# Layer 1's turned parts prepared ahead of its loop, and layer 3's third products in groups of nine blocks

## The chip, the core and the metric

The kernel runs on one core of one Trainium2 chip. The metric is the device time of one execution in microseconds; lower is better. Five engines run their own instruction streams beside each other: PE (matrix multiplication), DVE (vector), ACT (scalar functions), POOL (GpSimd) and SP, which here only issues DMAs. They wait for one another through semaphores.

## What is computed

Four graph layers over 3327 nodes (padded to 3328 = 26 blocks of 128) with 64 features, and one adjacency matrix `adj`; after each, `x = layernorm(x + layer(x))`. The kernel gets `adj` transposed, so a block is 128 rows of it. The two layers that the change touches:

```python
# layer 1
x_tan = _logmap0(x, C)
adj_att = jax.nn.sigmoid(x_tan @ att_W[:D] + att_b + (x_tan @ att_W[D:]).T) * adj
x_local = _logmap(x[:, None, :], x[None, :, :], C)
support_t = jnp.einsum('ij,ijd->id', adj_att, x_local)
return _proj(_expmap(x, support_t, C), C)

# layer 3
support = input @ weight
mask = (adj != 0).astype(support.dtype)
rank = jnp.cumsum(mask, axis=1)
deg = rank[:, -1:]
k = jnp.minimum(deg, float(MAX_NEIGH))
pos = rank - (deg - k)
w = mask * jnp.where(pos > 0, DECAY ** (k - pos), 0.0)
return w @ support + bias
```

## The kernel before

**Layer 1** (`near_sphere`, the arm that runs for this input). The distance of every pair of nodes comes from a product of two turned matrices: `ljT` (64 features on the partitions, nodes along the row; two copies, `ljT[1]` with the two halves of the partitions exchanged) and `riT`. Both are made by PE transposes into PSUM and a copy from there; `right` turns blocks of `lj` for `ljT[0]`, `turn` turns blocks of `ri` for `riT`, and `change_over` copies finished blocks of `ljT[0]` into `ljT[1]` by two DMAs on SP. A call such as `right, 1, 4` does blocks 1 to 4.

The loop runs over 104 tiles: two passes `cp` over the columns, 26 blocks `jb` in the order of `order`, two chunks `ci` of 2 x 416 columns. For a tile t, `products(t)` (L1103) writes four matmuls to a PSUM buffer `pq`, of which there are three, each of two banks; `linear(t)` lets DVE make `a` (L1115) from it and the attention `sg`, and ACT square it in place (L1116); `gather(t)` lets DVE make `v` (L1124), frees `pq` with that, issues `products(t + 3)` and adds v's product to an accumulator (L1136). Every second tile, `attention` lets ACT make a pair's sigmoids (L1076) and POOL multiply them with the adjacency block (L1088); SP loads that block (L1058, four buffers). Pass 0 also makes one block's factors on ACT per pair (`rows_of_sums`, L1230). The order on PE, ACT, DVE and POOL is the order of the program text (`manual_schedule`).

[...] Ahead of the loop six belong to single-use tiles (`alone`), and afterwards to the three `pq` buffers; two are the accumulators' (`bank(0, ...)`, `bank(1, ...)`), which serve for preparation first. Four parts are not prepared ahead but in the loop, at tiles 13 and 25: `gather` calls `prepare`, which takes the next `pq` buffer of the ring, does the transposes, and leaves the two copies to ACT one tile later.

**Layer 3** (in `layers`). Each step q is a block of one half h of the columns (52 steps, from the last block to the first). `masks` makes 0/1 masks on DVE three steps ahead (L341) from half a block each, loaded by SP into four buffers `ah` (L339). `advance` lets PE count neighbours along the blocks by four matmuls per c (L526); `read` turns the counts into weights `w`, for c = 0 on ACT (L541) and for c = 1 on DVE (L539). `products` multiplies w with the node features, which are split into three bf16 parts: the first two stand side by side in `s12` and take full-width matmuls (L722); the third, `s3`, is 64 columns wide, and its matmuls (L737) run in pairs, one for each half of the array's columns. The third products are not issued with each block: `later` collects blocks and issues them for `GROUP` = 3 blocks together, in the lines

```python
if last or c and len(later) == 2 * GROUP:
    for ql, cl in later:
```

At a half's last block, what is left is issued first for c = 0, then for c = 1. Until its third product is done, a block's w must stay; each c has `LEAD + GROUP + 2` buffers for it. `LEAD` = 3 is how many steps `products` stays behind `read`. The half's end (`sums_out`, `half_out`) normalises the first half's result on DVE and ACT, one part per step, beside the first steps of the second half.

Of the kernel before, what the change touches and what calls it, by code (L numbers as in the profile page):

```python
# [10 lines left out]
F32 = mybir.dt.float32  # L11
# [8 lines left out]
P = 128  # L20
N = 3327
NB = 26
# [41 lines left out]
CUBIC_PLUS = 2 * CUBIC_ROOT - 1  # L64
CUBIC_REST = 1.75705840270866
NEIGH = 100
GROUP = 3
LEAD = 3
AHEAD = 3
STEP = float(2**7)  # L70
# [6 lines left out]
def kernel(  # L77
# [819 lines left out]
    with tc.tile_pool(name="l1", bufs=1) as l1:  # L897
# [20 lines left out]
        with tc.tile_pool(name="l1a", bufs=1) as l1a, tc.tile_pool(  # L918
            name="l1ap", bufs=1, space=PSUM
        ) as l1ap:  # L920
            v = l1a.tile([P, NB], F32, name="v")
            sums = l1a.tile([P, NB], F32, name="sums")
# [26 lines left out]
            for i, g in enumerate(range(0, NBH, 4)):  # L949
                n = min(4, NBH - g)  # L950
# [60 lines left out]
        def near_sphere(mT, ljT_0, xm, sq_e, t_e, rows_63):  # L1011
# [3 lines left out]
            with tc.tile_pool(name="n1", bufs=1, reuse_waits="tile") as n1, tc.tile_pool(  # L1015
# [45 lines left out]

                orders = (order, sorted(order, key=lambda jb: jb in kept))
                tiles = [(cp, jb, ci) for cp in range(2) for jb in orders[cp] for ci in range(2)]
                us, pqs, a_s, accs, copies, sums = {}, {}, {}, {}, [], []

                def attention(pair):

# [26 lines left out]
                def products(t):  # L1094
                    if t >= len(tiles):
                        return
                    cp, jb, ci = tiles[t]
                    ch = 2 * cp + ci
                    of = slice(jb % NBH * P, (jb % NBH + 1) * P)
                    pq = n1q.tile([P, 2, 512], F32, tag="pq", name=f"pq_{t}")[:, :, :CW]  # L1100
                    for h in range(2):
                        rows = slice(h * D, (h + 1) * D)
                        nc.tensor.matmul(  # L1103
                            pq[:, h, :], ljT[h != jb // NBH][rows, of],
                            riT[rows, ch * CW : (ch + 1) * CW], start=True, stop=True,
                        )
                    pqs[t] = pq

                def linear(t):

                    if t >= len(tiles):
                        return
                    one = slice(slot(tiles[t][1]), slot(tiles[t][1]) + 1)
                    a_s[t] = n1w.tile(TW, F32, tag="a", bufs=3, name=f"a_{t}")
                    stt(a_s[t], pqs[t], CUBIC_PLUS, us.pop(t), op0=ALU.add, op1=ALU.mult)  # L1115
                    nc.scalar.activation(  # L1116
                        pqs[t], pqs[t], AF.Square, bias=al[:, one], scale=ga[:, one]
                    )

                def gather(t, extra=()):  # L1120

                    cp, jb, ci = tiles[t]
                    w = n1w.tile(TW, F32, tag="v", name=f"v_{t}")
                    stt(w, pqs.pop(t), CUBIC_REST, a_s.pop(t), op0=ALU.add, op1=ALU.mult)  # L1124
                    while sums:
                        sums.pop(0)()
                    if extra:
                        copies.extend(prepare(f"t{t}", extra))
                    if not extra:
                        products(t + 3)  # L1130
                    if jb == orders[cp][0]:
                        accs[cp, ci] = n1c.tile(
                            [P, CW], F32, tag=f"acc{ci}", name=f"acc1_{cp}_{ci}"
                        )
                    for h in range(2):
                        nc.tensor.matmul(  # L1136
                            accs[cp, ci][h * D : (h + 1) * D, :], xv[:, slot(jb), :], w[:, h, :],
                            start=(jb == orders[cp][0]), stop=(jb == orders[cp][-1]),
                        )
                    if extra:  # L1140
                        products(t + 3)
                    if jb == orders[cp][-1]:
                        of = slice((2 * cp + ci) * CW, (2 * cp + ci + 1) * CW)
                        sums.append(lambda: nc.scalar.copy(mT[:, of], accs[cp, ci]))
                        if t + 1 == len(tiles):
                            while sums:
                                sums.pop(0)()
# [43 lines left out]
                def change_over(b, n):  # L1191
                    of = slice(b * P, (b + n) * P)
                    nc.sync.dma_start(ljT[1][D:, of], ljT[0][:D, of])
                    nc.sync.dma_start(ljT[1][:D, of], ljT[0][D:, of])
# [7 lines left out]
                        )  # L1202
                    return riT[:, b * P : (b + n) * P], pt[:, : n * P]

                def prepare(name, parts):

                    pt = n1q.tile([P, 2, 512], F32, tag="pq", name=f"prep_{name}")
                    return [made(pt[:, k], *part) for k, part in enumerate(parts)]

                def made(pt, make, b, n):  # L1210
                    dst, src = make(pt, b, n)

                    def copy(to=nc.scalar.copy):
                        to(dst, src)
                        if make is right and b < 9:
                            change_over(b, n)

                    return copy

# [8 lines left out]
                def rows_of_sums(jb):  # L1228
                    sl = slot(jb)
                    nc.scalar.activation(  # L1230
                        xv[:, sl, : D - 1], xc[:, sl, : D - 1], AF.Copy, scale=gss[:, sl : sl + 1]
                    )

                def bank(which, make, b, n):

                    pt = n1c.tile([P, 4 * P], F32, tag=f"acc{which}", name=f"prep_{make.__name__}_{b}")
                    return made(pt, make, b, n)
# [3 lines left out]
                    pt = n1p.tile([P, 4 * P], F32, name=f"first_{make.__name__}_{b}")  # L1241
                    return made(pt, make, b, n)

                later = {13: ((right, 1, 4), (turn, 8, 4)), 25: ((right, 0, 1), (turn, 12, 1))}
                with tc.manual_schedule(
                    engines={
                        mybir.EngineType.PE, mybir.EngineType.Activation, mybir.EngineType.DVE,
# [49 lines left out]
                    n1q = pairs.enter_context(  # L1297
                        tc.tile_pool(name="n1q", bufs=3, space=PSUM, reuse_waits="tile")
                    )
                    by_rows = bank(1, left_rows, 0, NB)  # L1300
                    products(0)
                    products(1)
                    seventh = bank(0, right, 5, 4)
                    products(2)
                    list(attention(1))
                    rows_of_sums(order[0])
                    linear(0)
                    seventh()
                    list(attention(2))
                    for t in range(len(tiles)):  # L1310
                        linear(t + 1)
                        if t == 0:
                            by_rows()
                            rows_of_sums(order[1])
                        while copies:
                            copies.pop(0)()
                        gather(t, later.get(t, ()))
                        if t % 2 == 0:
                            list(attention(t // 2 + 3))
                            if t // 2 + 2 < NB:  # L1320
                                rows_of_sums(order[t // 2 + 2])
                        if t == 8:
                            spread_left(7)
                        if t == len(tiles) - 4:
                            of = slice(0, 2 * CW)
                            nc.gpsimd.tensor_tensor(xm[:, of], mT[:, of], ljT[0][:, of], ALU.mult)
                            gp = nc.gpsimd

                            gp.tensor_scalar(gs, g1, MIN_NORM, -256.0, ALU.max, ALU.mult)
                            gp.tensor_tensor(gk, gs, ga, ALU.mult)  # L1330
                            gp.tensor_scalar(gks, gk, -2.0, None, ALU.mult)
                            gp.tensor_tensor(gs2, gs, gs, ALU.mult)
                            gp.tensor_scalar(aav, aa, 1.0 / D, LN_EPS, ALU.mult, ALU.add)
                            gp.tensor_tensor(rows_63, but_last[:, :1], but_last[:, 1:], ALU.add)
                        if t == len(tiles) - 3:
                            pq = n1q.tile([P, 2, 512], F32, tag="pq", name="pq_early")
                            pm = pq[:, :, : 3 * (P + 2)].rearrange("p a (k w) -> p a k w", k=3)
                            for b in range(6):
                                nc.tensor.matmul(
                                    pm[:, b // 3, b % 3], mT[:, b * P : (b + 1) * P], all_m,  # L1340
                                    start=True, stop=True,
                                )
                        if t == len(tiles) - 2:
                            nc.scalar.activation(
                                sq_e.rearrange("p (a k h) d -> p a k (h d)", a=2, k=3),
                                pm[..., :P], AF.Square,
                            )
                            nc.scalar.copy(
                                t_e.rearrange("p (a k h) -> p a k h", a=2, k=3), pm[..., P:]
                            )  # L1350
# [521 lines left out]
```

## Time and profile before

| | us |
|---|---|
| median of 3 runs | 557.09 |
| lowest and highest | 556.18 and 557.86 |
| the profiled execution | 557.54 |
| its span in the profile | 555.7 |

| stage | us from the span's start |
|---|---|
| constants, layer 0 | 0 to 14 |
| layer 1: preparation | 14 to 22 |
| layer 1: loop of 104 tiles | 22 to 223 |
| layer 1: end | 223 to 241 |
| layer 2 | 241 to 394 |
| layer 3: node features, first steps | 394 to 409 |
| layer 3: steps, first half | 409 to 476 |
| layer 3: steps, second half | 476 to 541 |
| end | 541 to 556 |

Times in the profile are counted from the start of its span; 1.8 us of the execution lie outside it. A row of the time-ordered view has a start, a length, an engine, a line and what was written from what. PE's matmuls are pipelined, so the distance between two starts says what one costs, not its length. In brackets stands idle time of the engine before a row and what ended it.

### The profile page before, as it was taken

How to read it: one execution, taken by the hardware profiler on the slowest of the kernel's cores; microseconds unless marked ns; L12 is line 12 of the kernel's file. 1: busy time of each engine (PE TensorE's matmuls, PEld its weight loads, DVE VectorE, ACT ScalarE, POOL GpSimd, SP SyncE). 2: the span in 40 equal slices, each digit the busy share in tenths (PEclk: the TensorE clock that was granted, in tenths of full speed). 3: DMA queues.
4: the chain of work that ended last, by engine and by line, in shares of the span. 5: the costliest groups of instructions: out<-in, count | busy, mean ns of one | idle time of the engine just before them, and what ended most of it. 6: DMA issues, size and time to landing. Idle time of an engine off the chain costs nothing.

```text
span 555.7 us, 7392 instructions
## 1 busy us (share of the span) xinstructions
PE 527.5 (95%) x2841; PEld 226.9 (41%) x2841; DVE 372.2 (67%) x549; ACT 276.8 (50%) x325; POOL 207.4 (37%) x85
## 2 busy tenths in 40 slices
PE   8799989999999999999999999999999999999991
PEld 5422222222222222964444444434455555545541
DVE  6799999999999999798000011200678877887733
ACT  4899999999999997620000100000464333433321
POOL 3699999999999999000000000000001000000000
PEclk9889999999999999799999999999999999999996
DMA  8958866666667536799998049999029994799601
GB/s 282 365 205 288 257 209 225 210 223 220 225 232 243 187 123 247 277 416 425 423 427 367 1 163 424 426 426 399 6 66 344 329 326 167 246 296 349 247 1 38
DMA packets 33893, 143.57 MB, mean 258 GB/s; under 512 B 10269, under 2 KB 11959, under 8 KB 28855
## 3 DMA queue, kind: packets, MB, share of 16 engines
q1 hardware_dynamic: 31511, 142.40, 69.7%
q10 hardware_dynamic: 2336, 0.59, 0.5%
q8 instruction: 24, 0.39, 0.3%
q14 instruction: 22, 0.18, 0.1%
HBM read 141.53 MB, written 0.87 MB: 256 GB/s over the span
## 4 chain that ended last, share of the span: by engine, by line
PE 68%; DVE 17%; issue 7%; ACT 6%; POOL 1%; DVEq 0%; POOLq 0%; ACTq 0%
PE cnt L421 26%; PE cnt L526 11%; DVE v L1124 10%; PE pq L1103 9%; PE acc L722 6%; PE acc L1136 4%; PE acc L737 3%; ACT pq L1116 3%; ACT sg L1076 2%; DVE a L1115 2%; DVE w L539 1%; PE cnt L412 1%; DVE mask L341 1%; PE idle L928 1%; PE x_w L1455 1%
## 5 line engine op out<-in xcount | busy, mean ns | idle before, releaser
L1088 POOL TENSOR_TENSOR sg<-sg,at 128x1664 f32<-128x1664 f32 x44 | 163.7, 3738 | 3.7 <-ACT sg L1076 2.2
L1103 PE MATMUL pq<-riT,ljT 64*128 64x416 f32 x416 | 101.0, 564 | 11.6 <-DVE v L1124 7.9
L1116 ACT ACTIVATE pq<-pq,al,ga 128x832 f32<-128x832 f32 x104 | 104.6, 1012 | 12.1 <-DVE a L1115 12.0
L1115 DVE SCALAR_TENSOR_TENSOR a<-pq,sg 128x832 f32<-128x832 f32 x104 | 105.3, 1013 | 4.5 <-PE pq L1103 2.3
L1124 DVE SCALAR_TENSOR_TENSOR v<-pq,a 128x832 f32<-128x832 f32 x104 | 105.4, 1014 | 3.3 <-ACT pq L1116 2.2
L1136 PE MATMUL acc<-v,xv 128*64 128x416 f32 x416 | 96.0, 541 | 0.0
L1076 ACT ACTIVATE sg<-lb,rb 128x1664 f32<-128x1664 f32 (+1 forms) x53 | 87.3, 1649 | 0.0
L541 ACT ACTIVATE w<-cnt 128x832 int16<-128x832 f32 x55 | 47.3, 863 | 71.5 <-PE cnt L526 71.4
L421 PE MATMUL cnt<-at_l,lj 128*64 128x416 f32 x448 | 80.4, 513 | 0.0
L653 POOL TENSOR_TENSOR s<-sq,s 128x384 bf16<-128x384 f32 (+1 forms) x4 | 4.1, 1026 | 200.7 <-ACT s L652 200.7
L506 ACT ACTIVATE x<-cnt 128x416 f32<-128x416 f32 x8 | 4.1, 518 | 131.5 <-PE cnt L421 131.5
L539 DVE TENSOR_SCALAR w<-cnt 128x832 int16<-128x832 f32 x49 | 50.1, 1023 | 25.8 <-PE cnt L526 24.0
L1103 PEld LDWEIGHTS pq<-riT,ljT 64*128 64x128 f32 x416 | 31.7, 186 | 85.1 <-DVE v L1124 78.6
L526 PE MATMUL cnt<-mask,tri 128*128 128x416 bf16 x208 | 53.5, 339 | 0.1
L722 PE MATMUL acc<-w,s 128*128 128x416 bf16 x208 | 52.6, 339 | 0.5 <-DVE hid L794 0.5
L526 PE MATMUL cnt<-mask,rest 128*128 128x416 bf16 x200 | 51.6, 340 | 1.2 <-ACT w L541 0.6
L421 PEld LDWEIGHTS cnt<-at_l,lj 128*64 128x64 f32 x448 | 31.9, 137 | 46.2 <-issue 45.4
L1136 PEld LDWEIGHTS acc<-v,xv 128*64 128x64 f32 x416 | 20.7, 135 | 61.5 <-issue 57.8
L409 DVE COPY lj<-pn_l 128x512 f32<-128x512 f32 (+1 forms) x4 | 2.4, 592 | 61.6 <-PE pn_l L373 61.6
L341 DVE TENSOR_SCALAR mask<-ah 128x1664 bf16<-128x1664 f32 x42 | 43.4, 1034 | 0.0
L421 PE MATMUL cnt<-kept,lj 128*64 128x416 f32 x224 | 41.2, 513 | 0.0
L586 DVE TENSOR_TENSOR x<-x,xc 128x416 f32<-128x416 f32 x4 | 2.4, 588 | 41.5 <-ACT x L506 41.5
(285 smaller groups left out, 441.9 us busy)
## 6 DMA issues: line engine op xcount, KB each, us to landing
at_l<-in_adjT SPq DMA_DIRECT2D x24, 1664.0 KB, 12.8
at<-in_adjT SPq DMA_DIRECT2D x44, 832.0 KB, 4.9
ah<-in_adjT SPq DMA_DIRECT2D x42, 832.0 KB, 6.3
bt_l<-in_adjT SPq DMA_DIRECT2D x8, 1664.0 KB, 14.9
kept<-in_adjT SPq DMA_DIRECT2D x7, 1664.0 KB, 8.1
lb<-lf_rows SPq DMA_DIRECT2D x2, 384.0 KB, 6.1
ljT<-ljT SPq DMA_DIRECT2D x4, 128.0 KB, 5.5
x<-in_x ACTq DMA_DIRECT2D x1, 416.0 KB, 5.4
```

The source lines that it names most:

```text
L341: nc.vector.tensor_scalar(mask[q], at, 0.0, None, ALU.not_equal)
L421: nc.tensor.matmul(acc[c][h * D : (h + 1) * D, :], hw[:, slot(jb), :], blocks[jb][:, o : o + CW], start=c not in begun, stop=last, skip_gr ...
L526: nc.tensor.matmul(cnt[c][:, e, :], mat, mask[q][:, of], start=start, stop=(mat is tri), skip_group_check=True,)
L539: nc.vector.tensor_scalar(w.bitcast(I16), cnt[c], 0.0, None, ALU.max)
L722: nc.tensor.matmul(acc[h, c][:, e, :], s12[:, slot(jb)].rearrange("p t d -> p (t d)"), ws[q, c][:, e, :], start=first, stop=last,)
L1076: nc.scalar.activation(sg[:, :, of], lbs[:, :, of], AF.Sigmoid, bias=rb[:, sl : sl + 1])
L1088: nc.gpsimd.tensor_tensor(sg[:, :, of], sg[:, :, of], at[:, :, of], ALU.mult)
L1103: nc.tensor.matmul(pq[:, h, :], ljT[h != jb // NBH][rows, of], riT[rows, ch * CW : (ch + 1) * CW], start=True, stop=True,)
L1115: stt(a_s[t], pqs[t], CUBIC_PLUS, us.pop(t), op0=ALU.add, op1=ALU.mult)
L1116: nc.scalar.activation(pqs[t], pqs[t], AF.Square, bias=al[:, one], scale=ga[:, one])
L1124: stt(w, pqs.pop(t), CUBIC_REST, a_s.pop(t), op0=ALU.add, op1=ALU.mult)
L1136: nc.tensor.matmul(accs[cp, ci][h * D : (h + 1) * D, :], xv[:, slot(jb), :], w[:, h, :], start=(jb == orders[cp][0]), stop=(jb == orders[c ...
```

## The change

`GROUP` becomes 9, so that layer 3's third products are issued for nine blocks together, and each c has 14 buffers for w instead of 8.

In layer 1 the four parts that were prepared at tiles 13 and 25 are prepared ahead of the loop, and `prepare` and the `extra` path of `gather` go. `right, 0, 1` and `turn, 12, 1` share an accumulator's bank with the transposed row factors (`few`). `right, 1, 4` and `turn, 8, 4` take one `pq` buffer before the first product. All four are copied by DVE instead of ACT: `rows_1` and the two single blocks after `products(0)`, `rows_8` after `linear(0)`; `products(2)` moves behind it. Their `change_over` DMAs are issued at tiles 4 and 10.

```diff
-GROUP = 3
+GROUP = 9
...
-                def gather(t, extra=()):
+                def gather(t):
...
-                    if extra:
-                        copies.extend(prepare(f"t{t}", extra))
-                    if not extra:
-                        products(t + 3)
+                    products(t + 3)
...
-                    if extra:
-                        products(t + 3)
...
-                def prepare(name, parts):
-
-                    pt = n1q.tile([P, 2, 512], F32, tag="pq", name=f"prep_{name}")
-                    return [made(pt[:, k], *part) for k, part in enumerate(parts)]
-
-                def made(pt, make, b, n):
+                def made(pt, make, b, n, at_once=True):
                     dst, src = make(pt, b, n)
 
                     def copy(to=nc.scalar.copy):
                         to(dst, src)
                         if make is right and b < 9:
-                            change_over(b, n)
+                            if at_once:
+                                change_over(b, n)
+                            else:
+                                changes.append((b, n))
...
-                later = {13: ((right, 1, 4), (turn, 8, 4)), 25: ((right, 0, 1), (turn, 12, 1))}
...
-                    by_rows = bank(1, left_rows, 0, NB)
+                    few = n1c.tile([P, 4 * P], F32, tag="acc1", name="prep_few")
+                    by_rows = made(few[:, :P], left_rows, 0, NB)
+                    singles = [
+                        made(few[:, k * P : (k + 1) * P], make, b, 1, False)
+                        for k, make, b in ((1, right, 0), (2, turn, 12))
+                    ]
+
+                    fours_of = n1q.tile([P, 2, 512], F32, tag="pq", name="prep_fours")
+                    rows_1 = made(fours_of[:, 0], right, 1, 4, False)
                     products(0)
+                    rows_1(copy)
+                    for part in singles:
+                        part(copy)
+                    rows_8 = made(fours_of[:, 1], turn, 8, 4)
                     products(1)
                     seventh = bank(0, right, 5, 4)
-                    products(2)
                     list(attention(1))
                     rows_of_sums(order[0])
                     linear(0)
+                    rows_8(copy)
+                    products(2)
                     seventh()
                     list(attention(2))
                     for t in range(len(tiles)):
                         linear(t + 1)
                         if t == 0:
                             by_rows()
                             rows_of_sums(order[1])
-                        while copies:
-                            copies.pop(0)()
-                        gather(t, later.get(t, ()))
+                        gather(t)
...
+                        if t in (4, 10):
+                            change_over(*changes.pop(0))
```

## Prediction, before the run

> **What bounds the kernel now.** I read the page's slices first, then the time-ordered rows of each stage the change touches, then the waits there.
>
> ```profile
> PE   8799989999999999999999999999999999999991
> DVE  6799999999999999798000011200678877887733
> ACT  4899999999999997620000100000464333433321
> POOL 3699999999999999000000000000001000000000
> ```
>
> A slice is 13.9 us. Up to 222 us (layer 1) all four engines stand at nine tenths; afterwards only PE does. So layer 1 must be read by who waits for whom, and layer 3 (from 392 us) first as a sum of PE's slots.
>
> Layer 1, all engines around tile 13 (columns: start, us, engine, line, operation):
>
> ```profile
> 52.49 1.01 DVE L1115 SCALAR_TENSOR_TENSOR a<-pq,sg 128x832 f32<-128x832 f32 x1
> ...
> 52.63 0.65 PE L1175 MATMUL prep_t<-ident,lj 128*128 128x128 f32 x4
> ...
> 53.12 0.60 PE L1199 MATMUL prep_t<-ident,mT 128*128 128x128 f32 x4
> 53.61 1.02 DVE L1124 SCALAR_TENSOR_TENSOR v<-pq,a 128x832 f32<-128x832 f32 x1
> ...
> 54.48 0.59 ACT L1214 COPY ljT<-prep_t 128x512 f32<-128x512 f32 x1
> ...
> 54.69 1.89 PE L1103 MATMUL pq<-riT,ljT 64*128 64x416 f32 x8
> 54.96 0.59 ACT L1214 COPY riT<-prep_t 128x512 f32<-128x512 f32 x1
> ...
> 55.78 1.02 DVE L1115 SCALAR_TENSOR_TENSOR a<-pq,sg 128x832 f32<-128x832 f32 x1 [1.15 <-PE pq L1103]
> ```
>
> DVE runs a, v, a, v without a gap, 0.93 us apart, until `prep_t` takes the `pq` buffer that tile 16's products should have had. They go only at 54.69, after the next v has given up a buffer, and DVE stands 1.15 us. The same happens at 80.00 (1.13 us).
>
> Is something behind DVE that would keep it from going earlier? POOL:
>
> ```profile
> 131.88 70.75 POOL L1088 TENSOR_TENSOR sg<-sg,at 128x1664 f32<-128x1664 f32 x19 [0.52 <-ACT sg L1076]
> ```
>
> From 132 us on POOL multiplies without a gap, 3.72 us a pair, exactly DVE's pace (4 x 0.93).
>
> Layer 3, PE and then DVE:
>
> ```profile
> 430.86 0.52 PE L722 MATMUL acc<-w,s 128*128 128x416 bf16 x2
> 431.31 1.25 PE L737 MATMUL acc<-w,s 128*64 128x416 bf16 x12
> 432.49 0.52 PE L526 MATMUL cnt<-mask,rest 128*128 128x416 bf16 x2
> ```
>
> ```profile
> 485.20 1.07 DVE L798 TENSOR_REDUCE v_out<-sq 128x8 f32<-128x512 f32 x2
> 486.19 1.02 DVE L539 TENSOR_SCALAR w<-cnt 128x832 int16<-128x832 f32 x1
> ...
> 489.49 1.02 DVE L539 TENSOR_SCALAR w<-cnt 128x832 int16<-128x832 f32 x1
> ...
> 494.23 1.02 DVE L539 TENSOR_SCALAR w<-cnt 128x832 int16<-128x832 f32 x1
> 495.16 1.02 DVE L341 TENSOR_SCALAR mask<-ah 128x1664 bf16<-128x1664 f32 x1
> 497.32 1.03 DVE L539 TENSOR_SCALAR w<-cnt 128x832 int16<-128x832 f32 x1 [1.15 <-PE cnt L526]
> ```
>
> Full-width matmuls start 0.1757 us apart. From the last L722 to the second L526 after a burst of third products lie 1.63 us; two neighbours' steps and six pairs at that pace are 8 x 0.1757 = 1.41. So a visit costs 0.23 us beside its work, and a burst of three blocks 6 x 0.1757 + 0.23 = 1.28 us. The DVE rows show the other thing: from 484 to 496 us, where the first half's result is normalised, DVE has no gap while PE has some.
>
> **What the Trainium skill says.** "TensorEngine Tiling (Array Packing)", Tiling Modes, Key Properties: changing the tiling mode drains the TensorE, and different tiles work in parallel. The trace agrees on both: 0.23 us a visit, and L737's pairs start 0.003 us apart. "SBUF — State Buffer", Who interferes with whom: DVE and GpSimd share a port pair that one holds exclusively. The trace shows it in layer 3 (a mask of 1.02 us took 1.72 beside POOL's `s3` at 411) but not for DVE's copies out of PSUM (0.69 us beside POOL at 20.25, as elsewhere). "TensorE: Matmul & The Clock Gate", Architectural detail: ACT and DVE work strictly in order, so what is queued behind a stalled operation stalls too.
>
> **Layer 1's part.** Removed from the loop: two visits to the `pq` ring, ten transposes, four ACT copies, two pairs of DMAs. The pace without a visit is 7.65 us for four tiles (a at 42.99 and 50.63, and again from 93 us on). With one: 46.91 to 55.78 is 8.88, then 7.71; 71.14 to 80.00 is 8.86, then 7.72. Excess 1.23 + 0.06 + 1.21 + 0.07 = 2.57 us, never made good afterwards. What is late next: POOL's multiply ends 0.6 us before a of tile 14; POOL needs 7.4 us for four tiles where DVE needs 7.65, so its lead grows. From 20.21 to 217.48 POOL has 193.7 us of work (163.7 + 22.3 + 7.7), so 3.6 us of gaps: it could end 3.6 earlier, and 2.57 is less. ACT loses its copies, nothing more. I take 2.57 (ends 1.3, if POOL holds the first half back, and 2.9).
>
> Added ahead of the loop. PE: by_rows, two single transposes, four for `rows_1`, then products(0). PE is free at 20.05 and products(0) started at 20.31; seven transposes at 0.11 us put it at some 20.8, done by 21.8; a of tile 0 starts at 22.20, because POOL's first multiply ends then. DVE: `rows_1` (0.69, as the row at 20.25) and two 128-wide copies (0.29 each, as L1592's 128-wide form, an estimate) go into 20.94 to 22.20, 1.26 us idle; `rows_8` (0.69) into the 0.89 between the first two a. products(2) waits for that copy: 23.9 to 24.9, needed at 26.02, when POOL frees tile 2. Behind products(2) on PE stands only the seventh bank's transposes, whose copy ACT takes at 24.27; if PE puts them behind, ACT is up to 0.4 us late. Then a of tiles 4 and 6 begin 0.04 and 0.07 us after POOL, which no edit moves. I take 0.1 us lost (ends 0 and 0.6). The four DMA issues on SP (0.53 to 0.60 each) move to tiles 4 and 10; what is queued behind them are loads that land about 5 us after issue and have 11 us (three pairs of POOL); their data is first needed at tile 29. Nothing.
>
> **Layer 3's part.** Bursts per half: eight of three blocks and, at the last block, two small ones for its two pairs of chunks (4 matmuls each); then two of nine blocks and two of 16 matmuls. Twelve visits fewer, 12 x 0.23 = 2.7 us, if PE sets the time everywhere. It does not. A step without burst is 12 x 0.1757 = 2.11 us of PE; DVE's share is w and mask, 1.88, and PE needs w 1.07 us after w's start, which leaves 0.14 us. DVE's other work sat under the bursts:
> - Steps 5 to 11 (s3's remainders 0.47 and 0.60, x3 0.47 and 0.60, by the steps in the row). The bursts at steps 5 and 8 go. Following both engines from row to row: w of step 6 starts at 417.12 instead of 416.89, where PE would have it; of step 9 0.37 late; of step 10 0.20 late, because the mask before it waits 0.3 beside POOL's `s3`. Less the room of 0.14, PE loses 0.09 + 0.23 + 0.07; of 0.46 saved, 0.1 is left.
> - Steps 12 to 20 and 21 to 28: two visits fewer each, 0.46 and 0.46, less 0.11 where step 26 has the short counts.
> - Steps 30 to 38 (bursts at 32 and 35 go, 12 pairs = 2.11 us more at 38). Step 32: DVE is the chain from 484.26 to 496.1, so the 1.28 us saves nothing. Step 35: w at 494.23 + 1.07 = 495.30 instead of PE's 496.41, 1.11 saved. Net 2.11 - 1.11 = 1.0 lost.
> - Steps 39 to 47 and 48 to the end: 0.46 each. At the end ACT's L752 lies ahead of PE's end, and its wait goes: 541.42 to 541.13, 0.29.
>
> Sum 0.1 + 0.46 + 0.35 - 1.0 + 0.46 + 0.46 + 0.29 = 1.1 us gained. Against it the mask loads:
>
> ```profile
> DMA to landing us min/median/max: 4.7/6.3/10.9
> ```
>
> A load is issued as a mask ends and needed four steps later: 4 x 2.11 - 1.04 = 7.4 us without a burst between. Loads issued at 509.03 and 511.14 took 7.9 and 7.6. I take 0.3 us lost (ends 0 and 1.5). The larger w ring (14 tiles for 8) moves addresses; the first `ah` loads have 27 us of slack, so nothing. Layer 3: 0.8 gained (from -0.7 to 1.4).
>
> **Sum.** 2.57 - 0.1 + 0.8 = 3.3 us. The profiled execution took 557.54 (span 555.7 and 1.8 around it), so 554.2; it lies 0.45 above the median of the three, 557.09, so 553.8.
>
> **Rivals.**
> - Layer 3 gives PE's whole saving, 2.7 + 0.3, as if DVE's work found room: 551.6. For it: PE at nine tenths throughout. Against: the DVE rows at 484 to 496.
> - DVE's stretches cost more, or half the mask loads come late: layer 3 loses 1 us: 555.6. For it: 0.14 us of room a step.
> - POOL holds layer 1, which gains 1.3: 555.1. For it: 0.6 us of lead at tile 14. Against: the lead grows.
> - Slower: the mask stream becomes the bound between bursts. From 430 to 440 us the DMA engines are 97% busy at 344 GB/s; 832 KB take 2.48 us so, 2.4 without the idle 3%, against 2.11 a step. Over some 20 burst-free streaming steps, 0.3 each is 6 us: 557.1 - 3.6 + 6 = 559.5. The gain is gone at 2.29 us a load. Against: landings at 501.34, 503.38 and 505.38, 2.0 us apart, and four loaded buffers after each burst.
>
> **How the numbers follow.** Forecast 0.46, whole saving 0.12, layer 3 loses 0.19, POOL 0.13, mask stream 0.10. A measurement here tells 0.3% (1.7 us) from nothing: below 555.4 is faster. That takes the first two, most of POOL's and 0.05 of the third: 0.72; same 0.18; slower 0.10. The forecast's own range is 553.0 to 554.8; with the costs' ends and the third case, 552.0 to 556.2.
>
> **What would show it.** No `prep` rows after 26 us, a of tile 16 near 54.5, DVE without waits for products in layer 1, its last v near 220; L737 in four bursts of 36 matmuls and four of 16 instead of twenty visits; DVE gapless from the half's turn to the 9-block burst. Wrong if DVE's stalls stay at tiles 14 to 30, POOL's row becomes gapless from 20 us, or masks wait for `ah`.

## The result and the profile after

The changed kernel takes 553.67 us (median of 7 runs, 552.95 to 554.55), the kernel before 557.25 beside it (7 runs, 556.18 to 559.13): a ratio of 0.9938, 95% interval 0.9925 to 0.9951. The prediction said 553.8. The profiled execution took 554.5 us, its span 552.8.

The page's slices of the changed kernel (40 of 13.8 us, busy tenths):

```profile
PE   8879999999999999999999999999999999989991
DVE  6789999999999999899000011200679769697733
ACT  4699999999999997620000100000365333433321
POOL 3599999999999999000000000000001000000000
```

The row of PE hardly tells the two kernels apart; in layer 3 DVE's digits now go up and down with the bursts. The gain has to be read by stage. Layer 1 first, DVE in order of time around tile 14 (a at 52.97), where it had stood 1.15 us before:

```profile
52.97 1.01 DVE L1115 SCALAR_TENSOR_TENSOR a<-pq,sg 128x832 f32<-128x832 f32 x1
53.90 1.01 DVE L1124 SCALAR_TENSOR_TENSOR v<-pq,a 128x832 f32<-128x832 f32 x1
54.83 1.01 DVE L1115 SCALAR_TENSOR_TENSOR a<-pq,sg 128x832 f32<-128x832 f32 x1
55.94 1.02 DVE L1124 SCALAR_TENSOR_TENSOR v<-pq,a 128x832 f32<-128x832 f32 x1
56.88 1.01 DVE L1115 SCALAR_TENSOR_TENSOR a<-pq,sg 128x832 f32<-128x832 f32 x1
```

and the groups of DVE between 26 and 223 us (busy us and mean ns of one, then idle time before them and what ended it):

```profile
L1124 DVE SCALAR_TENSOR_TENSOR v<-pq,a 128x832 f32<-128x832 f32 x103 | 104.4, 1013 | 3.4 <-ACT pq L1116 2.3
L1115 DVE SCALAR_TENSOR_TENSOR a<-pq,sg 128x832 f32<-128x832 f32 x103 | 104.2, 1011 | 0.0
```

No a waits for products any more; in the kernel before its row, over the same stretch, was

```profile
L1115 DVE SCALAR_TENSOR_TENSOR a<-pq,sg 128x832 f32<-128x832 f32 x102 | 103.3, 1013 | 2.4 <-PE pq L1103 2.3
```

with 2.4 us of idle time, 2.3 of it ended by PE's products. From a of tile 14 to a of tile 16 it is 3.91 us instead of 5.15.

Layer 3, PE in order of time around step 38, then DVE from the first half's end to that burst:

```profile
498.58 0.52 PE L722 MATMUL acc<-w,s 128*128 128x416 bf16 x2
499.03 3.36 PE L737 MATMUL acc<-w,s 128*64 128x416 bf16 x36
502.32 0.53 PE L526 MATMUL cnt<-mask,rest 128*128 128x416 bf16 x2
```

```profile
480.64 1.02 DVE L539 TENSOR_SCALAR w<-cnt 128x832 int16<-128x832 f32 x1 [1.32 <-PE cnt L526]
...
482.51 1.07 DVE L798 TENSOR_REDUCE v_out<-sq 128x8 f32<-128x512 f32 x2
483.50 1.01 DVE L539 TENSOR_SCALAR w<-cnt 128x832 int16<-128x832 f32 x1
...
486.80 1.02 DVE L539 TENSOR_SCALAR w<-cnt 128x832 int16<-128x832 f32 x1
...
491.54 1.01 DVE L539 TENSOR_SCALAR w<-cnt 128x832 int16<-128x832 f32 x1
...
497.73 1.02 DVE L539 TENSOR_SCALAR w<-cnt 128x832 int16<-128x832 f32 x1 [0.15 <-PE cnt L526]
499.72 1.03 DVE L341 TENSOR_SCALAR mask<-ah 128x1664 bf16<-128x1664 f32 x1 [0.97 <-DMA ah<-in_adjT]
503.23 1.02 DVE L539 TENSOR_SCALAR w<-cnt 128x832 int16<-128x832 f32 x1 [2.48 <-PE cnt L526]
```

None of the four w from 483.50 to 491.54 (steps 32 to 35; the third is at 489.27) has a bracket: DVE is late, not PE. They stand at the same distances as before (486.19, 489.49, 491.96, 494.23), although PE has lost a burst of 1.28 us between them; only behind step 35, where the second burst went, are 1.12 us won. The work of both comes back at 499.03 as a longer burst, beside which DVE waits 2.48 us.

The profiled executions by stage (differences between starts of rows, for DVE's last row its end; "L2" is layer 2's first product, "w3" DVE's w of step 3):

| stage | before | after | difference |
|---|---|---|---|
| span's start to a of tile 8 | 39.26 | 41.60 | +2.34 |
| a of tile 8 to the last v | 184.06 | 181.44 | -2.62 |
| last v to L2 | 17.80 | 16.39 | -1.41 |
| L2 to w3 | 169.11 | 169.03 | -0.08 |
| w3 to w12 | 23.16 | 23.01 | -0.15 |
| w12 to w21 | 22.84 | 22.38 | -0.46 |
| w21 to w29 | 20.42 | 20.11 | -0.31 |
| w29 to w39 | 28.28 | 29.26 | +0.98 |
| w39 to w48 | 22.84 | 22.38 | -0.46 |
| w48 to the end of DVE's last row | 20.61 | 19.88 | -0.73 |
| from there to the end | 7.34 | 7.28 | -0.06 |

Two large entries, +2.34 and -1.41, stand where the prediction had put 0.1 and nothing. That is what most of the repeats below are about.

### The profile page after: what moved, and what is told of

The parts are those of the page before. It is cut to its first block, busy times and chain, and to the rows that moved or that the text cites. A ratio compares the mean times of both kernels' runs of the same rounds, so it can differ in the third digit from the quotient of the medians.

```text
span 552.8 us, 7387 instructions
## 1 busy us (share of the span) xinstructions
PE 524.6 (95%) x2841; PEld 228.6 (41%) x2841; DVE 373.2 (68%) x553; ACT 275.2 (50%) x321; POOL 207.6 (38%) x85
## 4 chain that ended last, share of the span: by engine, by line
PE 66%; DVE 16%; ACT 11%; issue 5%; DVEq 0%; POOL 0%; ACTq 0%; POOLq 0%
PE cnt L421 26%; PE cnt L526 11%; DVE v L1124 8%; PE pq L1103 7%; PE acc L722 6%; ACT pq L1116 5%; ACT sg L1076 5%; PE acc L1133 4%; PE acc L737 3%; DVE a L1115 2%; DVE w L539 1%; DVE mask L341 1%; PE cnt L412 1%; PE idle L928 1%; PE pm L1416 1%
## 5 line engine op out<-in xcount | busy, mean ns | idle before, releaser
L539 DVE TENSOR_SCALAR w<-cnt 128x832 int16<-128x832 f32 x49 | 50.1, 1022 | 21.2 <-PE cnt L526 20.8
L1088 POOL TENSOR_TENSOR sg<-sg,kept 128x1664 f32<-128x1664 f32 (+1 forms) x10 | 30.0, 3026 | 0.8 <-ACT sg L1076 0.8
```

Source lines behind the costliest of these rows:

```text
L539: nc.vector.tensor_scalar(w.bitcast(I16), cnt[c], 0.0, None, ALU.max)
L1088: nc.gpsimd.tensor_tensor(sg[:, :, of], sg[:, :, of], at[:, :, of], ALU.mult)
```

## The experiments

Each edit is against the changed kernel unless its heading says otherwise.

**The two parts, each alone.**

```diff
 # layer 1's part alone
-GROUP = 9
+GROUP = 3
```

```diff
 # layer 3's part alone, against the kernel before
-GROUP = 3
+GROUP = 9
```

> The changed kernel with groups of three blocks in layer 3, as before: layer 1's part alone. My theory: layer 1's loop gives 2.6 us (two visits to the ring of products, 1.2 to 1.3 us each) and the start loses 0.1, so 2.5 us faster than the kernel before, about 554.7. Rival, the whole gain is layer 1's and layer 3 gives nothing: 553.6, as the changed kernel. Rival, the late first a (2.4 us later in the changed kernel's profile) is the change's own doing: every profile of this kernel has a of tile 0 near 24.7 us and the time is at most 0.3 us under the kernel before.

> The kernel before with groups of nine blocks: layer 3's part alone. My theory: 1.1 us faster than the kernel before, about 556.1, with 1.0 us lost between steps 29 and 39 and some 0.45 won in each other stage. Rival, PE alone sets the time: 3.0 faster, 554.2. Rival, mask loads come late between the bursts: no faster or slower. Start of layer 1: if the late first a comes from the phase of PE's clock window and not from the change, a of tile 0 may lie anywhere from 22.2 to 24.7 us here too, although nothing of layer 1 is changed.

Layer 1's part: 555.68 us, ratio 0.9967 (0.9948 to 0.9986). Layer 3's part: 556.62, ratio 0.9993 (0.9983 to 1.0004). Both gained less than expected. The traces don't agree with that: each stage is the changed kernel's where that part is in, and the old one's where it isn't. From a of tile 8 to the last v layer 1's part took 181.46 us and layer 3's 184.05; w29 to w39 28.28 and 29.27. From w3 to the end of DVE's last row layer 1's part took 138.15 us, as the kernel before did, and layer 3's 137.00, where the changed kernel took 137.02. What differs lies in the stretches without a changed instruction, and one load of layer 2 that was 0.7 us late. So both were run again, with the whole change beside them.

> The changed kernel once more, beside its two parts alone on one chip. Layer 1's part alone was 1.5 (+- 0.9) and layer 3's part alone 0.4 (+- 0.5) under the kernel before in the means, together 1.9, and both together 3.7. If the parts add up and this was spread: all three move to one sum, about 3.4 here, 2.5 and 1.0 for the parts. If something couples them (a part gives more in the other's presence): 3.5 here again and under 2.2 for the sum of the parts. Profile: from a of tile 8 to the last v 181.4 to 181.5 us, as in the four profiles with layer 1's part; a of tile 8 anywhere between 39.2 and 41.6.

> Layer 1's part alone, once more. Parts add up: 2.5 us under the kernel before. Coupled: 1.5 under it again. Profile: a of tile 8 to the last v 181.5; the stretch from the last v to layer 2's first product either 16.4 or 17.8 us, by where PE's half-speed window falls.

> Layer 3's part alone, once more. Parts add up: 1.1 us under the kernel before. Coupled, or layer 2's one late load of the first profile (0.7 us) belongs to this kernel: 0.4 under it again, with the wait for that load in the profile again. If that load was late by chance, the stretch from layer 2's first product to w of step 3 is 169.0 to 169.1 us, not 169.85.

The changed kernel: 553.9 us, ratio 0.9935 (0.9914 to 0.9956). Layer 1's part 555.9 (22 runs), 0.9970 (0.9958 to 0.9983). Layer 3's part 556.46 (22 runs), 0.9987 (0.9976 to 0.9997), and from L2 to w3 now 169.09: the late load did not come again. The medians are still not a clean sum: 0.30% and 0.13% against 0.65%. The lowest runs are: before 555.87 (of 82), layer 1's part 553.69 (of 31), layer 3's 554.71 (of 44), both 552.28 (of 15), which is 2.2 and 1.2 us, and 3.6 for both. Layer 1's part had 22 runs in the second set from 553.69 to 557.62, more than the loop's 2.6 us apart. Something worth over 2 us varies from one execution to the next; the next two runs name it.

**The start, in the kernel before.** No edit.

> The kernel before once more, for its start alone. If the late a of tile 8 (39.2 to 41.6 us in the ten profiles so far, three of them with the old layer 1 at 39.3, 40.2 and 39.5) comes from where PE's half-speed window falls, the old layer 1 shows 40.5 or more in some executions, with a window of 6.83 us from 12 to 22 us; if the changed start-up causes it, this stays at 39.2 to 40.2.

> The kernel before once more, for its start alone, as the run ahead of it: a of tile 8 at 40.5 us or later in some executions if it is the window's phase, always 39.2 to 40.2 if the changed start-up makes it late.

a of tile 8 began at 39.24 us in the one (an execution of 556.29 us) and at 40.57 in the other (557.32). The view of stretches shows PE from 16 to 20 us (length, busy us and instructions of PE, PEld, DVE, ACT, POOL, then the granted PE clock, DMA share, GB/s), first of the former, then of the latter, then of the changed kernel:

```profile
16.00:20.00 4.00, 3.78 (x35) 3.41 (x35) 3.86 (x10) 3.66 (x7) 0.00 (x0) 0.82 0.94 393
```

```profile
16.00:20.00 4.00, 3.50 (x18) 3.17 (x20) 3.96 (x10) 2.95 (x6) 0.00 (x0) 0.50 0.97 398
```

```profile
16.00:20.00 4.00, 3.38 (x16) 3.05 (x18) 3.96 (x10) 2.83 (x6) 0.00 (x0) 0.50 0.97 390
```

PE ran at half its clock through the whole stretch in the last two, and did 18 and 16 instructions in it instead of 35. The same unchanged instructions came out early or late. By the trace's clock records the half-speed stretch at the start is 3.41 us long in some executions and 6.83 in others, and so is the one near layer 1's end where there is one. The Trainium skill describes this: "TensorE: Matmul & The Clock Gate", Part 1, What's actually happening, says that PE's clock is halved or full by the activity in windows of 3413 ns, which don't begin with the kernel; lengths of one and two such windows agree. In all 14 profiles of this study every change of the clock lies a whole number of steps of 3.413 us behind the first half-speed stretch, up to 157 steps on. So the windows run on through an execution, and lie differently to its work each time.

The last unchanged instructions of PE ahead of the loop are four transposes (`first_turn`). All that comes up to the fourth of them is the same in both kernels. Sorted by the half-speed stretch (times in us):

| | half-speed stretch | fourth transpose starts | a of tile 8 | from the one to the other |
|---|---|---|---|---|
| old start, 3 profiles | 3.41 | 19.77 to 19.94 | 39.24 to 39.46 | 19.32 to 19.70 |
| old start, 1 profile | 6.83 (from 13.88) | 21.51 | 40.15 | 18.64 |
| old start, 1 profile | 6.83 (from 14.63) | 21.93 | 40.57 | 18.64 |
| new start, 2 profiles | 3.41 | 19.50, 20.13 | 39.17, 39.67 | 19.68, 19.54 |
| new start, 5 profiles | 6.83 (from 12.30 to 12.99) | 20.81 to 21.09 | 40.32 to 40.61 | 19.51 to 19.52 |
| new start, 2 profiles | 6.83 (from 14.49, 14.89) | 21.83, 22.09 | 41.34, 41.60 | 19.51, 19.52 |

So two things make up the +2.34. The fourth transpose came at 22.09 us instead of 19.94, before any changed instruction, as it came at 21.93 in the late profile of the kernel before: that is the clock's phase. And the changed part behind it costs 0.87 us (19.51 for 18.64) wherever PE comes late, so for that much the rival of layer 1's part alone is right: it is the change's own doing. In the old start with a short stretch PE was ready early, and a of tile 0 waited for POOL's first multiply, which ended at 22.14 to 22.37 us; there the added work is mostly hidden. With a long one PE sets the time, and every added transpose counts. PE, then DVE, of the changed kernel's profile (half speed until 21.72), then DVE of the late profile of the kernel before:

```profile
21.70 0.66 PE L1194 MATMUL first_turn<-ident,mT 128*128 128x128 f32 x4
...
22.52 0.60 PE L1170 MATMUL prep_fours<-ident,lj 128*128 128x128 f32 x4
23.23 0.97 PE L1103 MATMUL pq<-riT,ljT 64*128 64x416 f32 x4
24.13 0.65 PE L1194 MATMUL prep_fours<-ident,mT 128*128 128x128 f32 x4
```

```profile
24.75 1.03 DVE L1115 SCALAR_TENSOR_TENSOR a<-pq,sg 128x832 f32<-128x832 f32 x1 [0.50 <-PE prep_fours L1194]
```

```profile
23.42 1.02 DVE L1115 SCALAR_TENSOR_TENSOR a<-pq,sg 128x832 f32<-128x832 f32 x1 [0.48 <-PE pq L1103]
```

From the fourth transpose to the first products it is 1.15 us instead of 0.38, the price of the added transposes. a of tile 0 then starts 1.5 us behind the products instead of 1.1: its wait is put down to the second four transposes, which stand between products(0) and products(1). From there to a of tile 8 the new start wins back 0.3 us (16.86 for 17.15). All five old starts have a further half-speed stretch of 3.41 us in there, from 27.21 to 28.28 us on, and none of the nine new ones has; whether that is the 0.3 us isn't separated.

The last v to L2 took 17.80 us in the two profiles where a half-speed stretch of 6.83 us lay there (the kernel before and the first of layer 1's part alone), and 16.4 in the twelve others, with none or one of 3.41. Here too it is the phase. With the windows carried on from the start in steps of 3.413 us, one began between 5.83 and 7.70 us behind the last v in all five profiles that have a half-speed stretch there, and in none of the nine that have none (4.72 to 5.76, and the next from 8.13 on); 5.83 and 5.97 are the two with 6.83 us.

**The price of a visit in layer 1.** One visit to the ring of `pq` buffers at tile 60, nearly empty:

```diff
+def visit(t):
+    pt = n1q.tile([P, 2, 512], F32, tag="pq", name=f"visit_{t}")
+    right_of = by_half(lj)[:, 0].rearrange("p h d -> p (h d)")
+    nc.tensor.transpose(pt[:, 0, :P], right_of, ident)
+    copies.append(lambda: nc.scalar.copy(spare, pt[:, 0, :P]))
...
-    products(t + 3)
+    if t == 60:
+        visit(t)
+    else:
+        products(t + 3)
...
+    if t == 60:
+        products(t + 3)
```

> The changed kernel with one visit to the ring of products put into layer 1's loop at tile 60, which does nearly nothing (one transposition of 128x128, one copy of it to a tile that nobody reads); the output's computation is unchanged. My theory: it is the slot in the ring that costs, not the work in it, so from a of tile 60 to a of tile 64 (7.65 us without a visit) it takes 1.1 to 1.3 us longer, and that is never made good before the last v. Rival, the transpositions and copies cost, and eight of them stood at tile 13: 0.1 to 0.4 us. Rival, POOL holds the pace there and takes the stall up: nothing.

PE, then DVE, in order of time:

```profile
143.72 0.33 PE L1124 MATMUL visit<-ident,lj 128*128 128x128 f32 x1
143.97 0.92 PE L1143 MATMUL acc<-v,xv 128*64 128x416 f32 x4
145.58 1.93 PE L1104 MATMUL pq<-riT,ljT 64*128 64x416 f32 x8 [0.68 <-DVE v L1131]
```

```profile
144.51 1.01 DVE L1131 SCALAR_TENSOR_TENSOR v<-pq,a 128x832 f32<-128x832 f32 x1
146.62 1.02 DVE L1116 SCALAR_TENSOR_TENSOR a<-pq,sg 128x832 f32<-128x832 f32 x1 [1.10 <-PE pq L1104]
```

Four tiles took 8.64 us instead of 7.45 (7.65 in the expectation was the pace of the first tiles): 1.19 us for one transpose and one copy, as much as for the eight transposes at tile 13. It was never made good: a of tile 8 to the last v took 182.65 us against 181.44. The slot in the ring costs, not the work in it, and POOL, which multiplies without a gap from some 130 us on, doesn't take the stall up.

**Where the bursts stand.** In the second half, after blocks 28, 31 and 41 instead of 34 and 43:

```diff
-            if last or c and len(later) == 2 * GROUP:
+            full = q in (28, 31, 41) if q >= NB else len(later) == 2 * GROUP
+            if last or c and full:
```

> The changed kernel with the second half's third products done after blocks 28, 31 and 41 instead of 34 and 43 (one visit more), so that two short bursts of PE lie beside DVE's normalising of the first half, as in the kernel before. My theory (DVE sets the time from step 31 to 35, and the 9-block burst at 38 covers nothing): 1.0 to 1.3 us faster than the changed kernel, about 552.5. Rival, visits alone count: 0.2 slower, about 553.9.

552.49 us, ratio to the kernel before 0.9913 (0.9891 to 0.9935), 1.2 under the changed kernel, as the theory said: one visit more made the kernel faster. The intervals of the two kernels' times still overlap; the stages show it. w29 to w51 fell from 57.97 to 56.06 us, and 0.7 came back at the end, where ten blocks are left for the last bursts instead of eight.

**DVE's work under the burst.** The bursts stay, and the rest of the first half's normalising moves to step 38:

```diff
-            if first_out is not None and not turn:
-                next(first_out, None)
+            if q == NB + LEAD + 1:
+                next(first_out)
+            if q == NB + LEAD + GROUP:
+                list(first_out)
```

> The changed kernel with the rest of the first half's normalising (sums, root, the two multiplications, 3.4 us of DVE) put behind step 38's mask, beside the 9-block burst of PE. My theory: steps 31 to 35 fall from 10.9 to 8.4 us, and the burst hides the 3.4 us: 2.3 us faster than the changed kernel, about 551.4. Rival, the third burst's length is what counts and not DVE: no difference, 553.7. Rival, DVE's work makes the step behind the burst late: half of it lost, 552.5.

550.49 us (548.52 to 551.29), ratio to the kernel before 0.9877 (0.9858 to 0.9897). It beats both kernels. DVE in order of time, and PE's burst beside it:

```profile
480.52 1.02 DVE L539 TENSOR_SCALAR w<-cnt 128x832 int16<-128x832 f32 x1 [0.16 <-PE cnt L526]
...
482.63 1.02 DVE L539 TENSOR_SCALAR w<-cnt 128x832 int16<-128x832 f32 x1 [0.15 <-PE cnt L526]
...
484.74 1.02 DVE L539 TENSOR_SCALAR w<-cnt 128x832 int16<-128x832 f32 x1 [0.15 <-PE cnt L526]
...
495.18 1.07 DVE L798 TENSOR_REDUCE v_out<-sq 128x8 f32<-128x512 f32 x2
...
497.85 1.09 DVE L803 TENSOR_TENSOR hid<-hid,ln_r 128x512 f32<-128x512 f32 x2
498.86 1.02 DVE L539 TENSOR_SCALAR w<-cnt 128x832 int16<-128x832 f32 x1
```

```profile
494.48 3.36 PE L737 MATMUL acc<-w,s 128*64 128x416 bf16 x36
497.77 0.53 PE L526 MATMUL cnt<-mask,rest 128*128 128x416 bf16 x2
```

The brackets of 0.15 us are back, each w waits for PE, and steps go at 2.11 us. Of the normalising, 3.7 us long (495.18 to 498.86), all but the last 0.2 is hidden. w29 to w39 takes 27.13 us instead of 29.26. The profiled execution of 548.52 flatters it: it had the early start (39.17), and the end after DVE's last row took 5.73 us where all others took 7.2 to 7.7. The stage says 2.1 us less, w29 to w48 2.3.

Is it the burst beside it, or the piece being whole? The same piece two steps earlier, where no burst follows (against the kernel just above):

```diff
-            if q == NB + LEAD + GROUP:
+            if q == NB + LEAD + 7:
```

> As the kernel that puts the rest of the first half's normalising behind step 38's mask, but behind step 36's, where no burst follows. Theory, the cover by the 9-block burst is what pays: DVE's 3.7 us stand bare, steps 29 to 39 take 30.4 us instead of 27.1 (29.3 in the changed kernel). Rival, it pays to have the work in one piece instead of four: 27 to 28 us here too.

31.95 us from w29 to w39: 4.8 worse than under the burst and 2.7 worse than in four pieces. The cover is what pays. It is 1.5 more than expected, and PE's rows say why:

```profile
494.57 0.51 PE L526 MATMUL cnt<-mask,rest 128*128 128x416 bf16 x2 [1.78 <-ACT w L541]
...
497.00 0.69 PE L526 MATMUL cnt<-mask,rest 128*128 128x416 bf16 x2 [1.21 <-DVE w L539]
497.48 0.90 PE L526 MATMUL cnt<-mask,tri 128*128 128x416 bf16 x2
498.18 0.90 PE L722 MATMUL acc<-w,s 128*128 128x416 bf16 x2
498.87 0.90 PE L526 MATMUL cnt<-mask,rest 128*128 128x416 bf16 x2
```

```profile
493.00:497.00 4.00, 1.22 (x7) 0.58 (x7) 3.51 (x11) 1.83 (x3) 0.00 (x0) 1.00 1.01 417
497.00:501.00 4.00, 4.00 (x14) 1.70 (x15) 2.84 (x3) 0.44 (x1) 0.00 (x0) 0.57 1.05 295
```

(The second view is that of stretches, columns as above.) PE was busy 1.22 of 4 us, and from 497.19 its clock was halved for 3.41 us: pairs of matmuls then start 0.69 us apart instead of 0.35. At half speed these 3.41 us do the work of 1.7, enough for the 1.5. Without that it would be some 30.3 us (an estimate), still 3.1 over the 27.13 under the burst; but of the 2.7 over the four pieces only about 1 is the piece itself.

**The price of a visit in layer 3.** One block at a time:

```diff
-GROUP = 9
+GROUP = 1
```

> The changed kernel with third products of one block at a time (GROUP = 1): a visit in every step of layer 3. My theory, a visit costs 0.23 us and a pair 0.1757 us whatever the size of the burst: w of step 40 to w of step 48 lie 8 x (2.11 + 2 x 0.1757 + 0.23) = 21.5 us apart; DVE's normalising is then hidden, so the time is 46 visits x 0.23 less some 2.6 us of DVE's stalls, about 8 us over the changed kernel, 562. Rival, switching costs with each pair and not with each visit: 0.1757 + 0.04 a pair, 20.3 us for the same stretch.

```profile
506.11 0.52 PE L722 MATMUL acc<-w,s 128*128 128x416 bf16 x2
506.55 0.54 PE L737 MATMUL acc<-w,s 128*64 128x416 bf16 x4
507.03 0.53 PE L526 MATMUL cnt<-mask,rest 128*128 128x416 bf16 x2
```

w40 to w48 took 21.51 us, a step 2.69. With steps of 2.11 us without a burst, 3.39 with three blocks and 5.50 with nine, a burst costs 0.58, 1.28 and 3.39 us for 2, 6 and 18 pairs: 0.1757 a pair and 0.23 a visit at all three sizes. The execution took 560.1 us, not 562, but with an earlier start than the changed kernel's profile (39.67 against 41.60); without that difference 7.5 us over it, where 8 were expected.

## Why the prediction was right

- **The loop of layer 1, 2.57 us: measured 2.62**, and from 181.44 to 181.49 us in the eight profiles with the change and no visit, against 184.02 to 184.06 in the five without. The reason holds too: the visit's slot costs 1.2 us whatever its work. The rival that POOL holds the loop fell. Two signs announced in absolute times failed (a of tile 16 near 54.5 us, found at 56.88; the last v near 220, found at 223.04), because they took the start for fixed; the distances they were made from held.
- **The start, 0.1 us lost (0 to 0.6): too small.** The seven transposes were to put the first products 0.5 us later (20.8 for 20.31) and put them 0.77 later (1.15 for 0.38). What failed above all is that they were hidden under POOL's first multiply, with PE's arrival at 20.05 us taken as fixed. It came after 20.8 in seven of the nine profiles with the new start, and there the start lost 0.87 us; in the other two, 39.17 and 39.67 against 39.24 to 39.46, a few tenths at most. The wait of a of tile 0 for the second four transposes wasn't in the sum either. And the sum left out that the same code's start moves by 1.3 us between executions, more than any of its terms but the loop's. That seven of nine new starts and two of five old ones had the long stretch is too few to say that the change makes it likelier.
- **Layer 3, step by step:** steps 5 to 11 -0.1 (measured -0.15), 12 to 20 -0.46 (-0.46), 21 to 28 -0.35 (-0.31), 30 to 38 +1.0 (+0.98), 39 to 47 -0.46 (-0.46), to the end -0.75 (-0.73). The rival "PE's whole saving" would have had -0.46 from step 29 to 39 (two visits fewer); DVE's rows without a bracket show why not.
- **The mask loads, 0.3 us lost: measured nothing.** The slowest load took 8.3 us, and one mask waited 0.97 us for its load (499.72 above), but beneath the burst, where DVE stands idle anyway. w39 to w48 took nine steps of 2.11 and one burst of 3.39, exactly. So the rival with the mask stream as the bound fell, and layer 3 gave 1.1 us, not 0.8.
- **The sum.** The two sizes that were off have opposite signs: 0.3 that wasn't lost, and up to 0.8 more lost at the start. The profile's own difference, 3.0 us, is 2.62 of the loop and 1.13 of layer 3, less 0.9 net of the start (+2.34) and of the last v to L2 (-1.41), and some 0.1 more from layer 2 and the end. The mechanisms of the loop and of layer 3 held, but that the prediction came within 0.2 us of the median is luck, since the phase of PE's clock alone moves an execution by over 1 us at the start and by 1.4 at layer 1's end.

What stays open: why the medians of the parts alone add up to less (0.43%) than both together (0.65%). The stages in the traces do add up, and the gap of 0.22% is within what the three intervals leave open (0.27% together, an estimate). Some 0.2 us of it lies outside the span: layer 1's part alone took 1.94 us there on the mean of its 31 runs, where the kernel before took 1.74 and both parts 1.76. Longer half-speed stretches in the parts alone don't explain the rest. The clock on record with every run gives, as estimates, 19.6 us of half speed before, 16.9 with layer 1's part, 18.6 with layer 3's and 16.2 with both (standard errors of 0.3 to 0.8), and these differences do add up. Where in a run the stretches fell is known only from the profiles.

## What to carry to other kernels

A visit to a ring of buffers that the loop fills and empties in step costs the delay of the slot, however little is done in it: look whether preparation can go ahead of the loop. Work counted as hidden under another engine's is hidden only as long as its own engine arrives in time; ask what it costs when that engine is late. When PE's work is gathered into fewer and longer bursts, look first for what the short bursts were covering on the other engines, and move that work under the long ones; here that was worth another 2.1 to 2.3 us by its stage. Compare stages from row to row, not times from the span's start, when the start can move by more than the effect.

## What the runs showed of the hardware

- PE's half-speed stretches began and ended on one grid of 3.413 us through each of the 14 executions, which lay differently to the work each time. At the start a stretch came as 3.41 or 6.83 us with unchanged instructions, and the first part of layer 1 then lay up to 1.3 us later in the kernel before (39.24 to 40.57). Near layer 1's end a stretch of 6.83 us cost 1.4 us, and one of 3.41 us nothing.
- Short gaps of PE were enough for a half-speed stretch: two of 1.78 and 1.21 us, with PE busy 1.22 us of 4, were followed by 3.41 us at half speed in layer 3. And the profile need not show a gap: in the kernel before, PE is busy all through the 3.41 us ahead of the stretch at 229.15, from 226.99 on with matmuls of only two columns. The same instructions were followed by no such stretch in nine other profiles.
- The fixed price of a visit with half-width matmuls between full-width ones was 0.23 us for bursts of 4, 12 and 36 matmuls alike.
